# Conditioned residual product on one core: where W's second chunk is loaded, which square comes before which cast, and how the last stores are cut

## The chip, the cores and the metric

The kernel runs on one core of one Trainium2 chip. The metric is the device time of one execution in microseconds (us). Below, PE is the engine of the matrix products, PEld its weight loads, DVE the vector engine, ACT the scalar engine, POOL the GpSimd engine and SP the sync engine, which here issues only DMAs. ACT and POOL issue DMAs too. A queue of DMAs is named by the engine that issues into it.

## The reference

There are 8 batches b of 1024 rows with 512 columns (x), and one conditioning row of 512 for each batch. The reference computes, in this order:

```
ae    = layernorm(cond) * ln_g + ln_b
h     = gelu(ae @ w1 + b1)
xw    = h @ w2 + b2                    # 2 * 512 * 8 numbers a batch
layer = base + x_a @ x_b^T             # rank 8, per batch
x1    = 2 * x + x @ layer
ys    = cond / sqrt(512)
d     = rsqrt((ys*ys) @ (W*W) + 1e-8)
out   = x1 + ((x1 * ys) @ W) * d
```

Each batch is thus a chain of two 512x512 matrices that depend on the batch's conditioning row. The kernel multiplies the two together and applies the result to x.

## The kernel before

**Precision.** Most products are made of three: an operand is split into a rounded part (high) and what the rounding left (low), and high x high, high x low and low x high are summed in PSUM. So each operand needs a cast by ACT (the high part) and a subtraction by DVE (the low part) before it can be used.

**Stages.** (1) Setup, up to some 70 us: the conditioning path (layernorm, w1, gelu, w2, the rank factors), the factor d, and the products of base with the scaled W, the first of them for batch 0. (2) The main stage: 44 row tiles of x with the combined matrix, beside which PE makes the matrices of later batches. (3) The last two and a half batches, cut into blocks by a seven-product scheme (class `Seven`, method `part`). All operations of stages 1 and 3 are issued in the order that the program has: the wrappers `ve`, `se` and `sy` (line 64) and `mm` (line 44) pin DVE, ACT, SP and PE to it, and every operation made through a wrapper has the line of the helper in the profile (L62, L45). So the tile names have to tell them apart.

**The first 13 us, which the change touches.** Matrices of 512 rows are held as four chunks of 128 rows, k = 0 to 3.

- Loads (lines 89 to 97): ACT's queue gets W's chunk 0 (line 89) and, after one small activation, W's chunk 1 (line 124). SP's queue gets `small` (`sm`, line 90), chunks 0 and 1 of the transposed base (`b_raw`, lines 91 and 92), the conditioning rows (`cnd`, which live in `xab`, line 93), chunks 2 and 3 of W in one DMA, chunks 2 and 3 of base in one, then w1. In the text below, W0, W1, b0 and b1 are the first two chunks of W and of base.
- PE is kept busy with 11 products of zeros (`warm`, line 116) until data is there.
- POOL adds 2 to the diagonal of each base chunk (`twice_i`, line 156), so a cast of the diagonal block waits for POOL.
- ACT makes the high parts: `round_yw(k)` (line 147) that of W's chunk times ys, written to `nh`; `round_b(k)` (line 160) that of base, written to `bh`; and `square_w(k)` (line 166) the squares of W, written to `wsq`.
- DVE makes the low parts: `rest_yw(k)` writes `nl`, `rest_b(k)` writes `bl`. It also has the statistics of the layernorm (`st`, `mv`) and what follows them.
- The order on ACT and DVE is that of lines 180 to 210. After chunk 0, ACT has `round_yw(1)`, `round_b(1)`, the four squares, and `sd`, the square root of the variance (line 202). DVE has `rest_yw(1)`, `rest_b(1)`, `ysq` (line 196), the statistics (lines 198 and 200) and the Newton steps that need `sd`.
- PE's order (lines 264 to 305): 12 products of chunk 0 (`pg`: four column blocks c, three products each), then chunk 1 for c = 0 and 1 (six products: for each c the first reads `bh` and `nh`, the second `bh` and `nl`, the third `bl` and `nh`), then `pq_v`, the product of the squares, then chunk 1 for c = 2, then the transposes `pa` of the normalized conditioning rows, and so on.

**The end.** `Seven.part` (line 1005) runs seven block products in the order 1, 5, 6, 2, 7, 3, 4. In the very last call the blocks of product 4 (`sw`) are written in two pieces of 128 rows: for each piece, ACT copies 128x256 from PSUM into `o` (line 1034), and ACT's own queue stores it (line 1036). The store of product 7's block goes to SP's queue just before. `store` (line 1043) issues one DMA for each call.

DMA semaphores are eight lanes, which successive DMAs of SP and ACT take in turn; a DMA that takes up a lane waits until the lane's last one has landed.

Of the kernel before, what the change touches and what calls it, by code (L numbers as in the profile page):

```python
# [14 lines left out]
P = 128  # L15
# [3 lines left out]
KC = D // P  # L19
# [11 lines left out]
def cond_resid_kernel(ctx: ExitStack, tc: tile.TileContext, small, cond, condrows, consts,  # L31
# [32 lines left out]
    ve, se, sy = InOrder(nc.vector), InOrder(nc.scalar), InOrder(nc.sync)  # L64
# [14 lines left out]
    def big_tile(name, dtype=F32):  # L79
        return big.tile([P, KC, D], dtype, tag="big", name=name)  # L80


    w_sb = cp.tile([P, KC, D], F32, name="w_sb")
    b_raw = big_tile("b_raw")
# [3 lines left out]
    cnd, ae = xab[:NB, :], drow[:NB, :]  # L88
    se.dma_start(w_sb[:, 0, :], weight[:, 0, :])
    sy.dma_start(sm, small)  # L90
    for k in range(2):
        sy.dma_start(b_raw[:, k, :], baseT[:, k, :])
    sy.dma_start(cnd, cond)
    sy.dma_start(w_sb[:, 2:4, :], weight[:, 2:4, :])
    sy.dma_start(b_raw[:, 2:4, :], baseT[:, 2:4, :])
# [25 lines left out]

    root = cp.tile([NB, 1], F32, name="root")
    se.activation(root, eps_l, AF.Sqrt)
    se.dma_start(w_sb[:, 1, :], weight[:, 1, :])


    hT = sp.tile([P, KC, 2, 32], F32, name="hT")
# [19 lines left out]
    def round_yw(k):  # L147

        se.mul(n0[k][0], w_sb[:, k, :], ysT[:, k, 0:1])

    def rest_yw(k):
        h, l = n0[k]
        ve.scalar_tensor_tensor(l, w_sb[:, k, :], ysT[:, k, 0:1], h.bitcast(F32),
                                           ALU.mult, ALU.subtract)

    def twice_i(k):
        blk = b_raw[:, k, k * P:(k + 1) * P]
        pin(nc.gpsimd.tensor_tensor(blk, blk, two_i, ALU.add))

    def round_b(k, lo=0, hi=D, by=se.copy):  # L160
        (by(bh[:, k, lo:hi], b_raw[:, k, lo:hi]))

    def rest_b(k):
        ve.tensor_sub(bl[:, k, :], b_raw[:, k, :], bh[:, k, :].bitcast(F32))

    def square_w(k):
        se.activation(wsq[:, k, :], w_sb[:, k, :], AF.Square)
# [19 lines left out]
    rest_b(0)  # L187
    round_yw(1)
    twice_i(1)
    round_b(1)  # L190
    rest_yw(1)
    rest_b(1)
    for k in range(KC):
        square_w(k)
    ysr = ysT.unsqueeze(2).to_broadcast([P, KC, 4, NB])
    ve.tensor_mul(ysq, ysr, ysr)
    st = sp.tile([NB, 6], F32, name="st")
    ve.bn_stats(st, cnd)
    mv = sp.tile([NB, 2], F32, name="mv")
    ve.bn_aggr(mv, st)  # L200
    sd = sp.tile([NB, 1], F32, name="sd")
    se.activation(sd, mv[:, 1:2], AF.Sqrt, bias=eps_l)
    ve_l = sp.tile([NB, 1], F32, name="ve_l")
    ve.tensor_scalar(ve_l, mv[:, 1:2], 1.0, LN_EPS, ALU.mult, ALU.add)
    twice_i(2)
# [192 lines left out]
    rows = ppool.tile([P, KC, D], F32, tag="ph", name="rows")  # L398
# [506 lines left out]
    class Seven:  # L905
# [99 lines left out]
        def part(self, g, steps=(), last=False, then=None):  # L1005


            b, bank, steps = self.b, {}, iter(steps)
            o1, o2 = (pools["late"].tile([P, 2, D], F32, tag="o2", name=f"o{i}_{b}_{g}", bufs=4)
                      for i in range(2))  # L1010
            for p in self.ORDER:
                key = {5: "z", 3: "z", 2: "v"}.get(p, "w")

                def new(key, count=1):
                    pool, tag = (po, "po") if key == "z" else (acc, "acc")
                    bank[key] = [pool.tile([P, 2, HD], F32, tag=tag, name=f"s{key}{i}_{b}_{g}")
                                 for i in range(count)]

                if p in (1, 5):
                    new(key, 2 if p == 1 and last else 1)  # L1020
                self.product(g, p, bank[key], p in (1, 5))
                if p == 1:
                    new("v")
                o, cols = {1: (None, None), 2: (o1, slice(0, HD)), 3: (o1, slice(HD, D)),
                           6: (o1, slice(HD, D)), 4: (o2, slice(0, HD)), 5: (o2, slice(HD, D)),
                           7: (o2, slice(HD, D))}[p]
                for m, u in enumerate(bank[key]):
                    u, to = (u, slice(0, 2)) if len(bank[key]) == 1 else (u[:, 0:1], slice(m, m + 1))
                    if p == 1:
                        se.copy(bank["v"][0][:, to], u)  # L1030
                    elif p in (3, 7):
                        ve.tensor_add(o[:, to, cols], u, o[:, to, cols])
                    else:
                        se.copy(o[:, to, cols], u)
                    if last and p in (2, 3, 7, 4):
                        self.store(se if p == 4 else sy, o, g, int(p in (4, 7)), to, cols)
                    elif p in (3, 4):
                        self.store(sy, o, g, int(p == 4), to, slice(0, D))
                next(steps, None)
                if p == 7 and then:  # L1040
                    then()

        def store(self, queue, o, g, half, ms, cols):
            at = g * HT + 2 * P * half
            queue.dma_start(
                out[self.b, at + P * ms.start:at + P * ms.stop, cols].rearrange("(m p) d -> p m d", p=P),
                o[:, ms, cols])

    def late_pools():
        making.close()  # L1050
# [147 lines left out]
```

## Time and profile before

| what | value |
|---|---|
| median of 3 runs | 294.07 us (293.83 to 294.32) |
| the profiled execution's own time | 293.74 us |
| its span, from the first to the last instruction | 291.9 us |
| PE busy | 286.3 us, 98% of the span |
| DVE / ACT / POOL busy | 214.8 / 175.0 / 35.9 us |
| granted PE clock, mean | 0.998 |
| DMA | 62.14 MB, mean 213 GB/s |

"Busy" is the time in which an engine executes something; overlapping instructions count once. The page of the profile also shows the chain of work that ended last: it is followed from the last instruction back to whatever released each step, so what stands in it set the end, and what does not stand in it was hidden. The timeline gives one row for each instruction or merged group: start in us, duration in us, engine, line, operation, tiles as output<-inputs, shapes; in brackets the idle time of the engine before it and what ended that. A weight load (PEld) runs ahead of its product, about 0.23 us in a steady row of products. A DMA's row is its issue; when it lands is told by the time to landing.

### The profile page before, as it was taken

The numbers are of one execution on the slowest core, as the hardware profiler recorded it, in microseconds if no ns is written. First come the engines' busy times: TensorE is split into PE (matmuls) and PEld (weight loads), VectorE is DVE, ScalarE is ACT, GpSimd is POOL, SyncE is SP. The second block draws the span as 40 slices with busy tenths as digits, with TensorE's granted clock in tenths as the row PEclk, the third lists the DMA queues.
The fourth block names the chain that finished last, engine by engine and source line by source line (L and its number), as shares of the span: only waits on it lengthen the run. The fifth ranks groups of instructions, "written<-read, shape, count | busy, mean of one in ns | idle before, by whom it ended". The sixth has DMA issues, their size and how long they took to land.

```text
span 291.9 us, 4100 instructions
## 1 busy us (share of the span) xinstructions
PE 286.3 (98%) x1519; PEld 225.2 (77%) x1519; DVE 214.8 (74%) x295; ACT 175.0 (60%) x272; POOL 35.9 (12%) x77
## 2 busy tenths in 40 slices
PE   7999999999999999999999999999999999999995
PEld 3665566467877878888877888887888889999994
DVE  2889898989916999519799565326789977798912
ACT  5757263286849884658654575544658745856641
POOL 2111000202944560000022000000000000000000
PEclk9999999999999999999999999999999999999999
DMA  7999999992799783332328114262175870852334
GB/s 209 405 429 413 411 403 405 390 383 90 187 321 322 235 250 116 110 145 93 159 80 263 55 72 135 83 216 74 72 251 176 291 257 1 290 204 87 142 146 144
DMA packets 19924, 62.14 MB, mean 213 GB/s; under 512 B 2736, under 2 KB 4016, under 8 KB 15552
## 3 DMA queue, kind: packets, MB, share of 16 engines
q1 hardware_dynamic: 9504, 43.76, 40.7%
q10 hardware_dynamic: 6912, 12.32, 11.5%
q0 software_dynamic: 3488, 5.79, 7.5%
q8 instruction: 12, 0.20, 0.3%
q14 instruction: 8, 0.07, 0.1%
HBM read 44.02 MB, written 17.84 MB: 212 GB/s over the span
## 4 chain that ended last, share of the span: by engine, by line
PE 96%; DMA 2%; ACT 0%; DVE 0%; SPq 0%; ACTq 0%; issue 0%
PE po L45 42%; PE pp L45 20%; PE sw L45 9%; PE px L45 5%; PE sz L45 5%; PE pg L45 4%; PE pq L45 4%; PE sv L45 2%; DMA b_raw<-in_baseT 2%; PE pr L45 1%; PE pt_t L45 1%; PE ps_t L45 0%; PE pq_v L45 0%; PE pq_z L45 0%; ACT o L62 0%; DVE o L62 0%
## 5 line engine op out<-in xcount | busy, mean ns | idle before, releaser
L45 PE MATMUL po<-ph,xs 128*128 128x512 f32 x352 | 113.7, 392 | 0.0
L45 PEld LDWEIGHTS po<-ph,xs 128*128 128x128 f32 x352 | 66.0, 188 | 15.6 <-issue 1.7
L45 PE MATMUL po<-pl,xs 128*128 128x512 f32 x176 | 68.6, 390 | 0.0
L62 ACT COPY o<-po 128x512 f32<-128x512 f32 x44 | 25.9, 588 | 35.0 <-PE po L45 35.0
L45 PEld LDWEIGHTS po<-pl,xs 128*128 128x128 f32 x176 | 33.0, 188 | 6.7
L62 DVE TENSOR_TENSOR xs<-x,xs 128x1024 fp32r<-128x1024 f32 (+1 forms) x23 | 27.0, 1176 | 15.0 <-ACT xs L62 15.0
L62 DVE TENSOR_TENSOR nl_p<-n,nh_p 128x1024 fp32r<-128x1024 f32 x21 | 25.7, 1222 | 12.4 <-ACT nh_p L62 12.4
L62 ACT CAST nh_p<-n 128x1024 fp32r<-128x1024 f32 x21 | 22.1, 1054 | 14.6 <-DVE n L62 10.9
L62 ACT CAST xs<-x 128x1024 fp32r<-128x1024 f32 x22 | 23.0, 1056 | 3.6 <-DMA x<-in_x 3.6
L62 ACT COPY q<-pp 128x512 f32<-128x512 f32 x30 | 17.4, 586 | 8.7 <-PE pp L45 8.6
L542 POOL DMA_DIRECT2D fa<-kept_a x28 | 13.8, 508 | 58.3 <-PE pr L45 54.0
L45 PE MATMUL pp<-nh_p,sh 128*128 128x512 f32 x48 | 19.0, 396 | 0.0
L45 PE MATMUL pp<-nh_p,sl 128*128 128x512 f32 x48 | 18.7, 390 | 0.0
L45 PE MATMUL pp<-nl_p,sh 128*128 128x512 f32 x48 | 18.7, 390 | 0.0
L62 DVE SCALAR_TENSOR_TENSOR n<-w_sb,ysT,d 128x512 f32<-128x512 f32 x24 | 16.9, 748 | 0.9 <-DMA d<-d_out 0.9
L62 ACT CAST sh<-sraw 128x1024 fp32r<-128x1024 f32 (+1 forms) x14 | 12.9, 926 | 6.8 <-DVE sraw L62 6.8
L62 DVE TENSOR_TENSOR sl<-sraw,sh 128x1024 fp32r<-128x1024 f32 (+1 forms) x14 | 14.9, 1067 | 2.2 <-ACT sh L62 2.2
L62 DVE TENSOR_TENSOR pl<-q,ph 128x1024 fp32r<-128x1024 f32 (+1 forms) x10 | 11.1, 1116 | 6.9 <-ACT ph L62 6.9
L45 PE MATMUL px<-w,hT 128*32 128x512 f32 x128 | 15.6, 599 | 0.0
L62 ACT COPY o<-sw 128x512 f32<-128x512 f32 (+1 forms) x12 | 6.2, 518 | 15.4 <-PE sw L45 12.3
L62 DVE TENSOR_TENSOR q<-pr,q 128x512 f32<-128x512 f32 x14 | 8.8, 688 | 7.9 <-PE pr L45 7.8
L62 DVE TENSOR_TENSOR n<-n,n 128x1024 f32<-128x1024 f32 x12 | 14.5, 1225 | 0.1
(199 smaller groups left out, 576.6 us busy)
## 6 DMA issues: line engine op xcount, KB each, us to landing
w<-in_w SPq DMA_DIRECT2D x16, 1024.0 KB, 10.4
x<-in_x SPq DMA_DIRECT2D x16, 1024.0 KB, 5.6
out<-o ACTq DMA_DIRECT2D x44, 256.0 KB, 2.3
out<-o SPq DMA_DIRECT2D x8, 512.0 KB, 2.9
fa<-kept_a POOLq DMA_DIRECT2D x28, 64.0 KB, 2.7
ft<-kept_t POOLq DMA_DIRECT2D x28, 64.0 KB, 3.5
d<-d_out POOLq DMA_DIRECT2D x6, 256.0 KB, 7.3
w_sb<-in_w SPq DMA_DIRECT2D x1, 1024.0 KB, 8.5
```

The lines of the kernel that those rows point to most:

```text
L45: tc.keep_in_program_order(nc.tensor.matmul(*args, **kw))
L62: return lambda *a, **kw: pin(f(*a, **kw)) if InOrder.on else f(*a, **kw)
L542: nc.gpsimd.dma_start(fold[name, b][32 * c:32 * c + 32, :], kept[name, g][32 * i:32 * i + 32, :])
```

## The change

Three things are changed.

1. W's chunk 1 is no longer loaded through ACT's queue but through SP's, between chunk 0 and chunk 1 of base.
2. The squares of W's chunks 0 and 1 are placed on ACT in front of the cast of base's chunk 1; the other two follow after `sd`. On DVE, `rest_b(1)` is placed behind `ysq` and the two statistics instructions.
3. In the last call of `part`, each of the two stores of product 4 becomes two: rows 0 to 63 through ACT's queue, rows 64 to 127 through SP's.

```diff
     se.dma_start(w_sb[:, 0, :], weight[:, 0, :])
     sy.dma_start(sm, small)
-    for k in range(2):
-        sy.dma_start(b_raw[:, k, :], baseT[:, k, :])
+    sy.dma_start(b_raw[:, 0, :], baseT[:, 0, :])
+    sy.dma_start(w_sb[:, 1, :], weight[:, 1, :])
+    sy.dma_start(b_raw[:, 1, :], baseT[:, 1, :])
     sy.dma_start(cnd, cond)
...
     se.activation(root, eps_l, AF.Sqrt)
-    se.dma_start(w_sb[:, 1, :], weight[:, 1, :])
...
     round_yw(1)
     twice_i(1)
+    for k in range(2):
+        square_w(k)
     round_b(1)
     rest_yw(1)
-    rest_b(1)
-    for k in range(KC):
-        square_w(k)
     ysr = ysT.unsqueeze(2).to_broadcast([P, KC, 4, NB])
     ve.tensor_mul(ysq, ysr, ysr)
     st = sp.tile([NB, 6], F32, name="st")
     ve.bn_stats(st, cnd)
     mv = sp.tile([NB, 2], F32, name="mv")
     ve.bn_aggr(mv, st)
+    rest_b(1)
     sd = sp.tile([NB, 1], F32, name="sd")
     se.activation(sd, mv[:, 1:2], AF.Sqrt, bias=eps_l)
+    for k in range(2, KC):
+        square_w(k)
...
-                    if last and p in (2, 3, 7, 4):
-                        self.store(se if p == 4 else sy, o, g, int(p in (4, 7)), to, cols)
+                    if last and p == 4:
+                        for queue, rows in ((se, slice(0, P // 2)), (sy, slice(P // 2, P))):
+                            self.store(queue, o, g, 1, to, cols, rows)
+                    elif last and p in (2, 3, 7):
+                        self.store(sy, o, g, int(p == 7), to, cols)
...
-        def store(self, queue, o, g, half, ms, cols):
+        def store(self, queue, o, g, half, ms, cols, rows=slice(0, P)):
             at = g * HT + 2 * P * half
             queue.dma_start(
-                out[self.b, at + P * ms.start:at + P * ms.stop, cols].rearrange("(m p) d -> p m d", p=P),
-                o[:, ms, cols])
+                out[self.b, at + P * ms.start:at + P * ms.stop, cols].rearrange(
+                    "(m p) d -> p m d", p=P)[rows],
+                o[rows, ms, cols])
```

The order of PE's instructions is the same in both kernels.

## Prediction

> **What bounds the kernel now.** I read the page's head and its chain of work that ended last, then the list of PE's waits, then the chain in order of time, then the timeline of the first 16 us and of the last 5.
>
> ```profile
> span 291.9 us, 4100 instructions
> ...
> PE 286.3 (98%) x1519; PEld 225.2 (77%) x1519; DVE 214.8 (74%) x295; ACT 175.0 (60%) x272; POOL 35.9 (12%) x77
> ...
> PE 96%; DMA 2%; ACT 0%; DVE 0%; SPq 0%; ACTq 0%; issue 0%
> ```
> ```profile
> PE pg L45 <- ACT bh L62: 1.1, 1, 1.1
> PE warm L45 <- DVE eps_l L62: 1.0, 1, 1.0
> ```
> ```profile
> 1.16 4.56 DMA b_raw<-in_baseT
> ...
> 5.75 0.31 ACT bh L62
> ...
> 6.10 4.54 PE pg L45 x18
> ```
>
> PE is the bound. After its first real product at 6.10 us it waits for nobody, up to 288.37. So only three stretches can change the time: the 6.10 us ahead of PE's work, a new hole that the change tears into it, and the 3.5 us behind the last product. PE's order is unchanged, so a shift early on goes to the end one to one. The head is set by b0: it lands at 5.73 (1.16 + 4.56), ACT casts one block, PE starts.
>
> ```profile
> 5.75 0.90 ACT L62 CAST bh<-b_raw 128x128 fp32r<-128x128 f32 x3 [0.54 <-DMA b_raw<-in_baseT]
> 6.56 0.72 ACT L62 ACTIVATE nh<-w_sb,ysT 128x512 fp32r<-128x512 f32 x1
> 7.09 0.61 POOL L158 TENSOR_TENSOR b_raw<-b_raw,two_i 128x128 f32<-128x128 f32 x1 [0.77 <-DMA b_raw<-in_baseT]
> 7.31 0.93 DVE L62 SCALAR_TENSOR_TENSOR nl<-w_sb,ysT,nh 128x512 fp32r<-128x512 f32 x1
> 7.73 0.62 ACT L62 CAST bh<-b_raw 128x512 fp32r<-128x512 f32 x1 [0.45 <-POOL b_raw L158]
> 8.26 2.19 ACT L62 ACTIVATE wsq<-w_sb 128x512 f32<-128x512 f32 x4
> 8.38 0.69 DVE L62 TENSOR_TENSOR bl<-b_raw,bh 128x512 fp32r<-128x512 f32 x1
> 8.99 0.29 DVE L62 TENSOR_TENSOR ysq<-ysT 128x128 f32<-128x128 f32 x1
> 9.31 0.19 PEld L45 LDWEIGHTS pg<-nh,bl 128*128 128x128 f32 x1
> 9.54 0.40 PE L45 MATMUL pg<-nh,bl 128*128 128x512 f32 x1
> ```
>
> The reader is to see two things here. ACT idles 0.54 us for b0, and 0.45 us for POOL, which had waited for b1 (its landing: 1.63 + the median time to landing 5.4 = 7.03). And the first low part of chunk 1, `bl`, is done at 8.38 + 0.69 = 9.07, only 0.24 before PE loads it at 9.31.
>
> **Part 1, W1 on SP's queue.** Before, W1 shares the transfer engines with b0: ACT's queue issues it at 1.24 and it lands at 5.91 (its queue's two loads took 3.7 and 4.7 us), 0.18 after b0. After, it stands behind b0. W1 is 262 KB, and the transfer ran at some 385 GB/s between 3.75 and 5.5, so taking nearly all of it from ahead of b0 is worth up to 0.6 us: b0 at about 5.15. But ACT's `nh` of chunk 0 (4.49 + 0.72 = 5.21) then ends last; so the first cast starts at 5.24 in place of 5.75, and **PE starts 0.51 earlier**, at 5.59 (below: nothing gained, if b0 was slow for another reason; no more than 0.54, ACT's idle time). ACT loses an issue of 0.39 that lay beside its table load (nothing). SP gains an issue of some 0.42, so b1, `cnd` and chunks 2 and 3 are issued 0.42 later; they queue behind b0 anyway (issued at 1.63, landed at 7.03), and w1, issued at 4.42, waits for W0, not for these. b1 has the same bytes ahead of it as before, so I leave it at 7.03; W1, now with only b0, W0 and `sm` ahead, at 5.9 or before.
>
> **Part 2, the reorder.** ACT: casts 5.24, `nh` of chunk 1 at 6.56 - 0.51 = 6.05 to 6.77 (W1 must be there by then), two squares at 2.19/4 = 0.55 each to about 7.75, then the cast of b1 at 7.73 to 8.35: where it was, since POOL frees b1 at 7.09 + 0.61 = 7.70. The squares only fill ACT's wait. PE, 0.51 ahead, would load this `bh` at 8.85 - 0.51 = 8.34; it is ready at about 8.39: 0.05 lost.
>
> DVE: `nl` of chunk 1 at 7.31 - 0.51 = 6.80 to 7.73; then `ysq` and the two statistics, which took 8.99 to 10.07 = 1.08 us and overlap `nl` by 0.07: to 8.74; only then `bl`, 8.70 to 9.40. PE loads it at 9.43, in place of 9.31 - 0.51 = 8.80 that its early start would allow. After a stall a product follows its load by 0.1, not 0.23 (load at 11.57, the next product's start at 11.90 instead of 12.03), so the product starts at 9.54: **exactly as before**. The half microsecond of the head goes into DVE's new order. Bounds: if `nl` takes 0.75, as the `nl` at 5.24 did, `bl` starts 0.18 earlier, a gain of 0.18; the floor is `bl` right behind `bh`, ready at 9.07, loaded at 9.11, product at 9.21, a gain of 0.33. I take 0.0, since `nl` still runs beside POOL's addition, as it did when it took 0.93.
>
> After that: `sd` at about 8.8, then the last two squares when chunk 2 of W is there (9.19) to 10.36, against 10.45 before; `pq_v` needs all four at 10.57 or later: nothing. The layernorm's Newton steps move up by 1 us, but `pa` starts 0.09 after the product before it allows, as `pq_v` and `pq_z` do too; worth at most 0.09, put at 0.
>
> **Part 3, the end.**
>
> ```profile
> 287.69 0.38 SPq L62 DMA_DIRECT2D out<-o  x1
> 288.09 0.34 ACTq L62 DMA_DIRECT2D out<-o  x1
> 288.52 0.37 ACT L62 COPY o<-sw 128x256 f32<-128x256 f32 x1 [0.46 <-PE sw L45]
> 288.93 0.34 ACTq L62 DMA_DIRECT2D out<-o  x1
> ```
> ```profile
> 289.25:289.75 0.50, 0.00 (x0) 0.00 (x0) 0.00 (x0) 0.00 (x0) 0.00 (x0) 1.00 1.00 324
> ```
>
> The last column pair says: the 16 transfer engines are fully busy (share 1.00) at 324 GB/s while these stores run. The last store is issued at 288.93, its bytes move from 289.72, it lands at 290.65. Two halves move the same 128 packets of 1 KB through the same engines, about 0.39 us; SP is free from 288.07, so its half is issued at 288.93 too. The trace's wait records at the end show one side effect: SP waits for the eight lanes one after the other, 0.06 apart, and the last landing is on the second of them; with four stores it is on the fourth or third, so at least one wait fewer follows it: **-0.06**. Bounds: half the transfer saved, -0.19 and -0.12; or the halves queue behind each other as `sm` and W0 did, issued together at 0.74 with W0's first bytes 0.5 us after those of `sm`: +0.35, taking 0.0 as the value, by the row of the full engines.
>
> The Trainium skill speaks against this part ("DMA: Bandwidth & Descriptors", Rules for kernel authors): two transfers to disjoint partition halves serialize, since both spray over the same 16 engines, so use one transfer. By it the split is worth nothing; by half the transfer it would be -0.19. The share of 1.00 agrees with the page; whether the halves cost something extra no run here shows.
>
> **Sum.** 0.0 + 0.0 - 0.06 = -0.06 against the profiled execution: 291.9 becomes 291.8 of span, 293.74 becomes 293.68. The median shown, 294.07, is 0.33 above this execution; against it: **294.0 us**.
>
> **Rivals.** Each against 294.07; 0.2% (0.59 us) is about what a measurement of this kernel can tell from no change.
> - *The head start is kept.* `nl` takes 0.75 or DVE gets to `bl` sooner: -0.33 at most, the stores' halves -0.31 at most: 293.43. For it: ACT's idle 0.54 goes. Against it: DVE's row of five operations, and the full engines. Typically 293.7.
> - *Slower: b1 lands later behind W1.* The same SP queue now carries W1 between b0 and b1. With b1 d later, POOL, `bh` and `bl` move by d; it decides from `bh` done at about 8.68, a landing at 7.36 (d = 0.33); beyond, each us costs one. At the 250 GB/s that the transfers ran at from 6 to 7.5, 262 KB are 1.05 us: `bl` ready at 10.12, against 9.40: 0.72 lost, 294.7 after the lanes' 0.06. Against it: W1 was through before most of b1 in the old order as well.
> - *The change does not do what it says:* b0 lands no earlier (5.73). Then ACT is 0.51 later through two squares, `bh` ends at 8.86, `bl` runs 9.21 to 9.90 behind the statistics: 0.5 lost, 294.5.
>
> **How the numbers follow.** Forecast (within 0.25 of 294.0) 0.48; head start kept 0.25, of which 0.11 by over 0.2%; b1 late 0.17, of which 0.11 over; b0 not earlier 0.10, of which 0.06 over, for a stall there is not exact. So faster 0.11, slower 0.11 + 0.06 = 0.17, rounded with the stores' +0.35 to 0.19; same 0.70. The range takes in the head start kept whole, both lesser losses and most of the late b1: 293.4 to 294.7.
>
> **What would show it.** Right: first `pg` at about 5.6, `bl` of chunk 1 at about 8.7, the load of it released by DVE, `pq_v` near 10.57, last store landing 1.7 after its issue. Wrong: `bl` ready by 9.1 (faster); POOL's second addition after 7.5, or `nh` of chunk 1 waiting for W1 beyond 6.05 (slower); last landings over 2 us after the issue.

## The result, and the profile after

The changed kernel takes **295.77 us** (median of 19 runs, 294.51 to 298.04), the kernel before 293.99 (19 runs beside them, 293.75 to 294.56). The ratio is 1.0062, with a 95% interval of 1.0048 to 1.0075: slower by about 1.8 us. The forecast was 294.0, in a range that ended at 294.7. The times do not only lie higher, they also spread over 3.5 us, where those of before spread over 0.8.

The profiled execution took 294.96 us, against 293.74 before. It is among the faster ones of the 19, so it shows only part of the loss. The page's head and chain:

```profile
span 293.2 us, 4104 instructions
...
PE 287.6 (98%) x1519; PEld 225.4 (77%) x1519; DVE 215.2 (73%) x295; ACT 175.2 (60%) x272; POOL 36.2 (12%) x77
...
PE 95%; DMA 1%; DVE 1%; ACT 1%; issue 0%; ACTq 0%; DVEq 0%
```

And the list of PE's waits:

```profile
PE warm L45 <- DVE eps_l L62: 1.0, 1, 1.0
PE pg L45 <- ACT bh L62: 0.2, 1, 0.2
PE pg L45 <- DVE ve_l L62: 0.2, 1, 0.2
```

The reader is to see that PE's one long wait for `bh`, 1.1 us before, has become two short ones (0.2 + 0.2), and that DVE now has 1% of the chain (0% before). Yet the span is 1.25 us longer. Cutting it at the end of the last product (start + duration of PE's last row, 288.68 + 0.28) shows where:

| stretch | before | after | difference |
|---|---|---|---|
| up to the end of PE's last product | 288.37 | 288.96 | +0.59 |
| from there to the end of the span | 3.56 | 4.22 | +0.66 |

So both the head and the end lost, and the two differences make up the 1.25. One pair of executions fixes the first row only roughly: in `stores_only` below, whose head is that of before, PE's last product ended at 288.99 too. The second row is the same within 0.02 in all seven profiles of the changed kernel. This table is used for each run below.

### The profile page after: what moved, and what is told of

Read it like the earlier page. It is cut to its first block, busy times and chain, and to the rows that moved or that the text cites. A ratio compares the mean times of both kernels' runs of the same rounds, so it can differ in the third digit from the quotient of the medians.

```text
span 293.2 us, 4104 instructions
## 1 busy us (share of the span) xinstructions
PE 287.6 (98%) x1519; PEld 225.4 (77%) x1519; DVE 215.2 (73%) x295; ACT 175.2 (60%) x272; POOL 36.2 (12%) x77
## 4 chain that ended last, share of the span: by engine, by line
PE 95%; DMA 1%; DVE 1%; ACT 1%; issue 0%; ACTq 0%; DVEq 0%
PE po L45 41%; PE pp L45 20%; PE sw L45 9%; PE px L45 5%; PE sz L45 5%; PE pq L45 4%; PE pg L45 3%; PE sv L45 2%; DMA w_sb<-in_weight 1%; PE pr L45 1%; PE pt_t L45 1%; DVE bl L62 0%; PE ps_t L45 0%; PE pq_v L45 0%; PE pq_z L45 0%
```

## The experiments

Two theories were tested first. S: the split stores cost a fixed amount. H: the head costs more than predicted, and differently from run to run. All ratios are against the kernel before on the same chip; "end" is the second row of the table above.

### The parts by themselves

`stores_only` has only the split stores:

```diff
-                    if last and p in (2, 3, 7, 4):
-                        self.store(se if p == 4 else sy, o, g, int(p in (4, 7)), to, cols)
+                    if last and p == 4:
+                        for queue, rows in ((se, slice(0, P // 2)), (sy, slice(P // 2, P))):
+                            self.store(queue, o, g, 1, to, cols, rows)
```

> Only the stores are split; the loads and the order of the head are those of before. In the profile after the change, the stretch from the end of the last product to the end of the span grew from 3.56 to 4.24 us (+0.68). Theory S (two queues issuing at the same moment make both issues longer, 0.57 and 0.50 in place of 0.34, and the landing later, 2.21 us after the issue in place of 1.73): +0.7 us or more against the kernel before, and the times scatter from run to run as they do after the change (over 2 us). Rival theory H (the scatter and most of the loss come from the head): +0.7 us at most, and the times lie as close together as those of before (under 1 us).

Measured: 294.66 us (7 runs, 294.46 to 295.11), ratio 1.0025 (1.0014 to 1.0036). The end is 4.21 us. The fixed loss is in the stores, and it does not scatter.

`front_only` has the new load and the new order, with the stores of before.

> W's chunk 1 on SP's queue and the new order of ACT and DVE; the stores are those of before. Theory S: +0.6 us (the last product ended 0.59 us later in the profile after the change), little scatter. Theory H: +1.1 us or more, with a scatter of over 2 us, because the landings of the first loads differ from run to run.

Measured: 294.27 us (11 runs), ratio 1.0017 (0.9999 to 1.0035); ten runs lie between 293.52 and 294.75, one at 297.09. The loss is less than both theories said, and not clear of zero; there is a single stray.

`load_only` has only W1 on SP's queue:

```diff
+    sy.dma_start(w_sb[:, 1, :], weight[:, 1, :])
     sy.dma_start(b_raw[:, 1, :], baseT[:, 1, :])
...
     se.activation(root, eps_l, AF.Sqrt)
-    se.dma_start(w_sb[:, 1, :], weight[:, 1, :])
```

> Only W's chunk 1 moves to SP's queue; the order on ACT and DVE is that of before, where the low part of base chunk 1 stands ahead of the statistics. If the loss in the head came from the low part standing behind the statistics, this kernel is faster than the one with both front parts by 0.3 us or more, and about as fast as before or faster by up to 0.3 us. If it came from base chunk 1 landing later behind W's chunk 1, it is as slow as the one with both.

Measured: 294.17 us (12 runs), ratio 1.0014 (0.9995 to 1.0034); eleven between 293.74 and 295.04, one at 297.38. Its median is 0.1 below that of `front_only`, too close to tell the two apart. But the stray run was the profiled one: base chunk 1 landed at 9.41 us, not at 7.0. What that cost is told below.

`reorder_only` has only the new order on ACT and DVE.

> Only the order on ACT and DVE changes; W's chunk 1 stays on ACT's queue. PE starts at 6.1 us as before. Two squares ahead of the cast put it 0.5 us later, and the statistics ahead of the low part put that at about 9.9 in place of 9.07: +0.5 us if the order is the cause of the loss in the head; within 0.2 us of before if it is the loads.

Measured: 294.49 us (11 runs, 294.13 to 295.04), ratio 1.002 (1.0011 to 1.0028), as expected of the order: +0.5 us. `bl` of chunk 1 ran from 9.36 to 10.03 (it ended at 9.07 before). By itself the new order only costs; it is meant for an earlier start.

### Why the split stores are slow

`halves_on_sp` puts both halves on SP's queue (compared with `stores_only`):

```diff
-                        for queue, rows in ((se, slice(0, P // 2)), (sy, slice(P // 2, P))):
+                        for queue, rows in ((sy, slice(0, P // 2)), (sy, slice(P // 2, P))):
```

> Only the stores: both halves of each piece go to SP's queue, one after the other, and ACT issues none. If the +0.7 us of the split come from two queues issuing at the same moment (issues of 0.57 and 0.50 us, the landing 2.21 us after the issue), the issues are 0.34 us again, the second half is issued 0.4 us after the first, the landing is 1.7 us after that: +0.35 us. If a store of 64 rows is itself slow, the issues stay at 0.5 us or more and the loss at 0.7 us or more.

Measured: 295.38 us (5 runs), ratio 1.0047 (1.0034 to 1.0059), end 4.87. My own theory of that point, two queues issuing at the same moment, falls: nothing is simultaneous here and the issues are as long. The end is even longer, as four such issues now stand one behind another on SP. The rows of the stores to `out` in the last microseconds (the three numbers are the shortest, median and longest issue in ns), before and in this kernel:

```profile
L62 ACTq DMA_DIRECT2D out<-o x2: 338/338/338, 288.1 to 288.9; - x2
L62 SPq DMA_DIRECT2D out<-o x1: 383/383/383, 287.7 to 287.7; - x1
```
```profile
L62 SPq DMA_DIRECT2D out<-o x5: 383/553/587, 287.8 to 290.2; - x5
```

The 383 in both is the untouched store of product 7. Here a store of 64 rows takes about 0.55 us to issue; before, one of 128 rows took 0.34.

`whole_two_queues` keeps the pieces whole and gives the second to SP's queue:

```diff
-                        self.store(se if p == 4 else sy, o, g, int(p in (4, 7)), to, cols)
+                        self.store(se if p == 4 and m == 0 else sy, o, g, int(p in (4, 7)), to, cols)
```

> Only the stores: the pieces stay whole; the first is stored through ACT's queue, the second through SP's, so two queues are used, but never two issues at once and no halves. If the use of two queues near the end costs something in itself, +0.3 us or more. If only the simultaneous issue does, 0.0 us within 0.1.

Measured: 293.98 us (11 runs), ratio 1.001 (0.9989 to 1.0031), end 3.54. Two queues cost nothing at the end. (Two of its runs, 295.52 and 297.00, stray; they come up below.)

`halves_by_columns` cuts each piece by columns instead of rows:

```diff
+                        if p == 4:
+                            for queue, half in ((se, slice(0, P)), (sy, slice(P, HD))):
+                                self.store(queue, o, g, 1, to, half)
...
```

> Only the stores: each piece is again cut in two and stored through ACT's and SP's queues at the same moment, but by columns: 128 rows of 128 columns each, so the same bytes and the same number of stores as after the change, with 512 B in a row. Before and after the change, a store of 128 rows took 0.34 us to issue, one of 64 rows 0.47 to 0.59, on one queue or two. If the 64 rows are what is slow, the issues are 0.34 to 0.38 us here, and the loss is what the smaller pieces cost the transfer (packets of 512 B in place of 1 KB), 0.1 to 0.4 us. If any store of 64 KB, or two at once, is slow, issues of 0.5 us or more and +0.7 us.

Measured: 294.09 us (11 runs, 293.89 to 294.65), ratio 1.0005 (0.9996 to 1.0014), end 3.72. Same bytes, same number of stores, same two queues at the same moment, but 128 rows: the long issues are gone, and 0.16 us of the loss at the end is left (3.72 against 3.56), so it is the rows. The same rows of the changed kernel and then of this one:

```profile
L62 SPq DMA_DIRECT2D out<-o x3: 383/467/553, 288.3 to 289.8; - x3
L62 ACTq DMA_DIRECT2D out<-o x2: 498/535/572, 288.7 to 289.8; - x2
```
```profile
L62 SPq DMA_DIRECT2D out<-o x3: 332/383/419, 287.8 to 289.0; - x3
L62 ACTq DMA_DIRECT2D out<-o x2: 366/367/368, 288.2 to 289.0; - x2
```

How the 0.66 us comes about is in ACT's timeline after the change:

```profile
288.28 0.37 ACT L62 COPY o<-sw 128x256 f32<-128x256 f32 x1 [2.96 <-DVE o L62]
288.68 0.57 ACTq L62 DMA_DIRECT2D out<-o  x1
289.35 0.37 ACT L62 COPY o<-sw 128x256 f32<-128x256 f32 x1 [0.70 <-PE sw L45]
289.75 0.50 ACTq L62 DMA_DIRECT2D out<-o  x1
```

The first half-store holds ACT until 289.25 (288.68 + 0.57), past the end of PE's last product (288.96). So the second copy starts 0.39 after that product; before, the distance was 0.15 (288.52 against 288.37). That is 0.24. (The bracket names PE, but the copy follows the end of the issue by 0.10.) The last store then lands 2.21 us after its issue, where the last store of before took 1.73: another 0.48. From the last landing to the end of the span it is 1.22 us, before 1.28: SP's row of waits gives 0.06 back, as predicted. Sum: 0.24 + 0.48 - 0.06 = 0.66, as measured.

The transfer itself was slower too. A stretch of whole stores before and one of half-stores after (last two columns: busy share of the transfer engines, GB/s):

```profile
289.00:290.00 1.00, 0.00 (x0) 0.00 (x0) 0.00 (x0) 0.00 (x0) 0.00 (x0) 1.00 0.98 324
```
```profile
290.00:290.50 0.50, 0.00 (x0) 0.00 (x0) 0.00 (x0) 0.00 (x0) 0.00 (x0) 1.00 0.95 240
```

The engines are as busy and move a quarter less: packets of the same 1 KB took a median of 0.069 us in the half-stores, 0.047 in the whole ones. The Trainium skill's advice not to split a transfer by partition halves ("DMA: Bandwidth & Descriptors", Rules for kernel authors) was right in its direction; it says that the halves serialize and are not worth the trouble, and names no loss, where here they cost 0.66 us.

### Where the scatter comes from

`after_again` is the changed kernel, beside the others.

> The changed kernel once more, beside the others. Its parts cost +0.7 us (stores alone) and +0.3 us (head alone), together 295.0 us; its 19 runs had a median of 295.77 and went from 294.5 to 298.0. Theory A (the parts add up, and the rest is the head's scatter, of which those 19 runs had more than their share): a median of 294.9 to 295.2 with single runs over 296. Rival B (the parts together cost more than their sum): again 295.6 or more.

Measured: 294.73 us (11 runs, 294.48 to 297.81), ratio 1.0051 (1.0028 to 1.0075). Seven runs at 295.0 or below, four from 295.86 up. Rival B falls: the median is even a little under Theory A's 294.9 to 295.2, so the parts together cost no more than their sum, and the rest is scatter. These 11 runs and the first 19 differ by 1 us in the median all the same.

`w1_behind_b1` moves W1 to SP's queue too, but behind base chunk 1, with the order of before:

```diff
     sy.dma_start(b_raw[:, 1, :], baseT[:, 1, :])
+    sy.dma_start(w_sb[:, 1, :], weight[:, 1, :])
...
     se.activation(root, eps_l, AF.Sqrt)
-    se.dma_start(w_sb[:, 1, :], weight[:, 1, :])
```

> Only the load: W's chunk 1 on SP's queue, but behind base chunk 1; the order on ACT and DVE is that of before, as in the kernel with the load alone. If base chunk 1 lands late in some runs because it stands fourth in SP's queue, here W's chunk 1 takes that place, base chunk 1 lands before 6.6 us in the profile, and PE starts at 5.4 us; ACT then waits for W's chunk 1 until about 7.0, so +0.2 us, with W's chunk 1 late in some runs instead (single runs 1 us or more above the rest). If the queue's order has nothing to do with the scatter, no such runs or as many as with the load alone (1 of 12).

Measured: 293.97 us (11 runs, 293.54 to 295.03), ratio 1.0002 (0.9992 to 1.0012). In its profile b1 landed at 5.60 and W1 at 6.38, PE started at 5.29 and came to `pq_v` at 9.77, 0.80 ahead of before. Why this brings nothing is told below. One run, the 295.03, lies 1 us above the rest; one in eleven does not decide between the two readings.

`one_store_moved` is a control: the kernel before with one store of the main stage on SP's queue.

```diff
-        nc.scalar.dma_start(out[b, t * P:(t + 1) * P, :], o)
+        (nc.sync if (b, t) == (2, 3) else nc.scalar).dma_start(out[b, t * P:(t + 1) * P, :], o)
```

> A control for the scatter: the kernel before, with one store of the main stage (a tile of batch 2) moved from ACT's queue to SP's; head and end are those of before, and the store is hidden behind PE. Single runs 1 us or more above the rest were seen where W's chunk 1 was on SP's queue (5 kernels), and twice where only the last store had moved to SP's queue. If the number of DMAs on each queue is what brings them, they are seen here too (2 or more of 11 runs above 295.0 us). If they come from the loads of the head, none, and the median is that of before within 0.1 us.

Measured: 294.03 us (11 runs, 293.66 to 294.59), ratio 1.0002 (0.9993 to 1.001). No stray run, so nothing speaks for the number of DMAs on each queue; but 11 runs can easily miss strays as rare as one in eleven.

Five more executions of the changed kernel were profiled, to see its scatter in a trace.

> The changed kernel, one look, to see a slow run in a profile. If it is over 295.3 us: by the theory that the excess is a late landing in the head, its first product of base chunk 1 waits for the cast or the low part, and the landing of base chunk 1 is later than 7.1 us by about the excess over 294.7; by the rival, the excess stands at the end, in landings later than 2.2 us after the issue of the stores.

> The changed kernel, a second look for the same question, with the same two readings: an excess over 294.7 us in the landing of base chunk 1 (later than 7.1 us), or in the landings of the last stores (later than 2.2 us after their issue).

> The changed kernel, one look. Stores cost 0.67 us in every profile so far (the stretch from the last product to the end of the span was 4.21 to 4.24 us with them, 3.54 to 3.56 before). If this run is over 295.3 us: by the theory that the excess comes from late landings in the head, the end is again 4.2 us, and a landing of the first loads is later by about the excess; by the rival, the end is longer than 4.5 us; by a third, both are as before and PE waits somewhere between 25 and 286 us.

> The changed kernel, one more look for a slow run, with the same three readings: a late landing in the head with the end at 4.2 us, a longer end, or a wait between 25 and 286 us.

> The changed kernel, one more look for a slow run, with the same three readings: a late landing in the head with the end at 4.2 us, a longer end, or a wait between 25 and 286 us.

Measured, with the other two profiles of the same kernel, in the order of the last product:

| run | time | b1 lands | PE's last product ends | end |
|---|---|---|---|---|
| before | 293.74 | 7.03 | 288.37 | 3.56 |
| `after_again` | 294.48 | 6.98 | 288.49 | 4.21 |
| `after_look1` | 294.58 | 7.16 | 288.58 | 4.23 |
| `after_look2` | 294.91 | 6.96 | 288.91 | 4.22 |
| profile after | 294.96 | 7.11 | 288.96 | 4.22 |
| `after_look4` | 295.05 | 7.92 | 289.05 | 4.21 |
| `after_look5` | 295.32 | 8.33 | 289.32 | 4.22 |
| `after_look3` | 295.67 | 8.43 | 289.66 | 4.23 |

The end is the same in all seven, within 0.02 us, so their scatter lies ahead of the last product, and the three highest are those where b1 landed late. At `pa` (12.46 before) these three are 0.44, 0.84 and 0.94 late. The rest comes in small pieces later; in `after_look3` 0.28 of it stands at the products `pr` at 95 us, and `stores_only` has the same jump there with the head of before. The chain of `after_look3` up to 11.6 us, in order of time:

```profile
2.13 6.30 DMA b_raw<-in_baseT
8.43 0.07 issue
8.50 0.47 POOL b_raw L158
8.99 0.63 ACT bh L62
9.62 0.04 issue
9.66 1.92 PE pg L45 x6
```

The reader is to see b1 itself in the chain, issued at 2.13, landing 6.30 us later, then POOL, ACT and PE one behind the other with no slack. The trace has 16 completions for each of these DMAs, as many as there are transfer engines, and the DMA has landed with the last one: here fifteen came by 6.76 and one at 8.43. In `after_look5` four were late (7.11 to 8.33, the others by 6.67), in the stray run of `load_only` two (9.31 and 9.41, the others by 6.54).

That stray run shows how a late landing comes to cost more than its lateness. PE was out of work from 8.47 to 10.64, and its first product of chunk 1 came 1.57 later than before. But the last product of the run came 3.66 later. From 11.6 to 15.0 us the granted PE clock was half. The same stretch before and in this run (the third number from the end is the clock; the first bracket counts PE's products):

```profile
11.60:15.00 3.40, 3.40 (x26) 1.91 (x22) 3.30 (x11) 2.23 (x4) 0.00 (x0) 1.00 1.02 422
```
```profile
11.60:15.00 3.40, 3.40 (x12) 0.95 (x11) 2.74 (x10) 1.87 (x5) 0.87 (x2) 0.50 1.01 419
```

In that stretch the run lost another 1.5 us; 0.4 more came just before it, where PE waited for `bl`. The other executions over 297 us with W1 ahead of b1 on SP's queue (four) were not profiled, but their mean granted clock was 0.992 to 0.994 like this one's (0.993), and in all other runs of these kernels 0.996 or more.

`after_w1_on_act` is the changed kernel with the load alone undone.

> The changed kernel with its load undone: W's chunk 1 is on ACT's queue again, the reorder and the split stores stay. The reorder alone cost 0.5 us and the stores alone 0.7. If the load is what brings the scattered runs of the changed kernel (over 295.3 us in 17 of 32), this one has a median of 295.2 and stays within 0.7 us above it. If the reorder and the stores together scatter, single runs are 1 us or more above the rest, as with the whole change.

Measured: 295.09 us (5 runs, 294.70 to 295.44), ratio 1.0042 (1.0028 to 1.0056). The five stay within 0.39 of their median, with b1 landing at 6.77 in the profile. `after_look3`, `after_look4` and `after_look5` ran on the same chip beside it and had b1 late each time. Its median is what the new order (+0.5) and the half-stores (+0.66) make without the earlier start; it lies between the two medians of the changed kernel (294.73 and 295.77). Over all profiles: in the eight with W1 on ACT's queue, b1 landed at 6.77 to 7.58; in the nine with W1 ahead of it on SP's, at 6.96 to 9.41, four of them after 7.9. Together this points to the load on SP's queue, ahead of b1, as what brings the late landings. Five runs without a stray and four late landings of nine do not prove it.

Not settled: what holds one to four of the transfer engines up by 0.4 to 2.9 us, and why it came so unequally. Of the first 19 runs of the changed kernel 11 were over 295.7 (1 us more than the stores explain), of the 11 of `after_again` four; of the 23 runs of `front_only` and `load_only`, with the same load and whole stores, three were 1 us or more above the kernel before. And the two stray runs of `whole_two_queues`, whose head is that of before, were not seen in a profile. Their mean granted clock was 1.0; they may have another cause.

## Why the prediction was wrong

**What held.**
- *Part 1, the head start.* b0 was predicted at about 5.15 and PE's start at 5.59. In the seven profiles b0 landed at 4.95 to 5.42 and PE started at 5.32 to 5.85: 0.25 to 0.78 ahead of before.
- *Part 2, the gain goes into DVE's new order.* The chain of `after_again`, whose loads came as before:

```profile
6.81 0.66 DVE nl L62
7.48 0.47 DVE ysq L62
7.95 0.61 DVE st L62
...
8.68 0.67 DVE bl L62
...
9.41 1.19 PE pg L45 x4
```

  This is the row of operations that the prediction worked out: `bl` from 8.70 to 9.40, loaded at 9.43; measured 8.68 to 9.35, and PE goes on at 9.41. The product that starts then was put "exactly as before", at 9.54, and the last product of that run ended 0.12 us later than before. In this run, where nothing landed late, the head's 0.0 was right to about 0.1. Part of that was luck. The 0.0 rested on `nl` taking 0.93 beside POOL's addition; the run's rows show that it took 0.74, and that `ysq` behind it took 0.55 in place of 0.29:

```profile
6.74 0.74 DVE L62 SCALAR_TENSOR_TENSOR nl<-w_sb,ysT,nh 128x512 fp32r<-128x512 f32 x1
7.40 0.55 DVE L62 TENSOR_TENSOR ysq<-ysT 128x128 f32<-128x128 f32 x1
```

  The two errors nearly cancel.
- *The lanes.* One wait of 0.06 fewer, as said (1.28 to 1.22 us from the last landing to the end).

**What failed, first.** The step "taking 0.0 as the value, by the row of the full engines", for the half-stores, and its upper bound of +0.35. From a row of full engines I took the time of the bytes as given, whatever the cut. The row (289.25 to 289.75) also ends where the last store's bytes start, at 289.72: it shows the stores before, and in the two quarters of a microsecond after it the engines were 0.88 and 0.77 busy. No row of that trace showed what a store of 64 rows costs. The runs put +0.72 in its place (0.24 + 0.48): the issue is 0.13 to 0.23 us longer, it blocks ACT ahead of the second copy, and the landing is later. The sum had the last piece issued at 288.93 as before; the longer issue of the first piece, which stands in front of the last copy, has no term in it. With this fixed cost alone (`stores_only`, 294.66) the time was at the upper edge of the range.

**What failed, second.** The step "b1 has the same bytes ahead of it as before, so I leave it at 7.03". It landed at 6.96 to 8.43 in the seven profiles. The rival "b1 lands later behind W1" named the wait and its point of decision (a landing of 7.36) and got 0.17; the three runs beyond that point were 0.44, 0.84 and 0.94 us late at `pa`, for 0.56, 0.97 and 1.07 us of lateness beyond it. So its "each us costs one" held there, and its chance was too low. It did not hold in the run of `load_only`, where the half clock came on top. The reason that it gave, 1.05 us for W1's bytes, was not the mechanism: ten to fifteen of b1's sixteen completions came by 6.8 in the late runs too. What spoke against the rival, that W1 was through before most of b1 in the old order as well, is true of the bytes; it says nothing of the last of 16 engines, on which the landing depends.

**Smaller.** The other loads were left where they were, and they moved too. In the profile after, W0 landed at 4.67 (4.40 before), and DVE's whole row started 0.27 later; in `after_look1` W1 landed at 6.17 ("5.9 or before"). W's chunks 2 and 3 were left at 9.19; they landed at 9.09 to 10.06. In `after_look2`, with b1 on time, they landed at 9.59, and PE waited inside `pq_v` for the last square:

```profile
PEld pq_v L45 <- ACT wsq L62: 0.3, 1, 0.3
```

  It is the prediction's row on the squares ("nothing") that fails there: `pq_v` began 0.16 ahead of before, and `pa`, behind it, 0.24 late.

**The rival "the head start is kept" had a lower ceiling than I gave it** (-0.33 in the head). `w1_behind_b1` kept 0.80 us up to `pq_v`. It lost 0.33 inside `pq_v`, which waited for the last squares (W's chunks 2 and 3 landed at 8.89, ACT's two squares ran until 10.06):

```profile
10.12 0.14 PEld L45 LDWEIGHTS pq_v<-wsq,ysq 128*32 128x32 f32 x2 [0.20 <-ACT wsq L62]
```

It lost 0.06 at `pa`, which now waited for the layernorm (`drow` was done at 11.95, `pa` began at 12.06), and most of the rest between 39 and 45 us, where PE overtook the stream of w2. PE's weight loads in the window from 33 to 46 us there, a wait of which the same window of before has 0.3 us:

```profile
PEld px L45 <- DMA w<-in_w: 2.0, 3, 0.9
```

  Its last product ended 0.08 us before that of the kernel before. No kernel here clearly beats the one before. In this profile an earlier PE mostly waited longer, for the last squares and for the weights.

## What to carry to other kernels

Do not cut a short store by rows to use two queues before you have measured one such store; the cut by columns, with all 128 rows, avoided most of the loss here but gained nothing either (294.09 against 294.05 us). The issue of a DMA counts on the engine that issues it, so look at what stands behind it on that engine: here a longer issue delayed the last copy by 0.24 us. A load that PE waits for is as late as the last of 16 transfer engines (8.43, with fifteen done by 6.76), so price a change to the order of loads by the spread of landings too, not by its bytes alone. And before an early start is priced, look for the next wall behind it: in `w1_behind_b1` 0.80 us of lead at 5 us was 0.10 by 45 us, after a wait for the last squares and one for the weights' stream.

## What was not expected of the hardware

- At the kernel's end a store of 64 rows took 0.47 to 0.59 us to issue, one of 128 rows 0.33 to 0.42, whatever its bytes (64 KB in 64 rows: 0.55; 64 KB in 128 rows: 0.37; 128 KB in 128 rows: 0.34), and on SP's queue as on ACT's.
- Packets of 1 KB took 0.069 us in those stores, 0.047 in whole ones.
- One to four of the 16 transfer engines delivered their share of a 256 KB load 0.4 to 2.9 us after the others (8.43 against 6.76; 9.41 against 6.54).
- After PE had been out of work for 2.17 us (8.47 to 10.64), the granted clock was 0.50 from 11.6 to 15.0 us; after the 1.07 us of the kernel before it stayed at 1.00.
